# A fused four-layer attention kernel: the first batch of the one-head layer takes its weighted sums of values by seven products

## The chip, the cores and the metric

The kernel runs on one core of one Trainium2 chip. The time is the device time of one execution in microseconds (us); the smaller, the better. The program executes once on all four batches; each engine of the core (TensorE, called PE; VectorE, DVE; ScalarE, ACT; GpSimd, POOL; SyncE, SP, which issues the transfers) runs its own list of instructions in order and waits at semaphores for the others.

## The reference

Four layers follow one another on x of shape (4, 512, 32, 32), all in fp32: an 8-head self-attention, a linear attention with a gate, a 1-head self-attention over layer-normed input, and a 4-head self-attention over group-normed input. The change lies in the third, cut here to what it computes:

```python
def _L2_conv_ref(x, norm_w, w_qkv, b_qkv, w_proj, b_proj):
    xf = jnp.transpose(x, (0, 2, 3, 1)).reshape(b, h * w, c)      # 1024 tokens of 512 channels
    mu = jnp.mean(xf, axis=-1, keepdims=True)
    var = jnp.var(xf, axis=-1, keepdims=True)
    xn = (xf - mu) * jax.lax.rsqrt(var + EPS) * norm_w
    q, k, v = jnp.split(jnp.einsum('bnc,dc->bnd', xn, w_qkv) + b_qkv, 3, axis=-1)
    attn = jax.nn.softmax(jnp.einsum('bqc,bkc->bqk', q, k) * c ** (-0.5), axis=-1)
    out = jnp.einsum('bqk,bkc->bqc', attn, v)
    out = jnp.einsum('bnc,dc->bnd', out, w_proj) + b_proj
    return x + jnp.transpose(out.reshape(b, h, w, c), (0, 3, 1, 2))
```

## The kernel before

All of it is `plain_path`, which runs the layers in sequence and, inside a layer, the four batches. x of a batch is a tile of 128 partitions x 4 channel chunks x 1024 tokens (2 MB). [...] `away(b)` (L573) stores a batch, `back(b)` (L576) fetches one into the tile that the store has freed. Both are issued by SP, in program order.

**Seven products.** A 2 x 2 block matrix product normally takes eight products of quarter size. `seven_products` (from L711) does it with seven, p1 to p7, at the price of sums of quarters: s1 to s4 of the stationary side (made by POOL in `sum_weights`, L693), t1 to t4 of the moving side (made by DVE in `sum_inputs`, L683), and sums of the results, which DVE takes out of PSUM (lines 737, 739, 774, 780). After p1 and p2 of all outputs `o`, it goes through pairs of outputs in the order p6(a), p7(a), p6(a+1), p5(a), p4(a), p7(a+1), p3(a), p5(a+1), p4(a+1), p3(a+1), and after every second one it calls `slot()`. A call `slot()` takes one entry off the list `pieces` and runs it: this is how work of another stage is put between products. `flush()` runs what is left at once.

**The one-head layer, per batch.** (1) q is projected; (2) v is projected (`project_v`: seven slots); (3) `one_head` computes the scores with keys first (`seven_products` with four outputs: ten slots, no slot in its p1 and p2), `exp` (L1237) on ACT, and a running sum `acc` of the exponentials on DVE (L1240); (4) `one_head` computes the weighted sums of values, divides by the row sums (`row_sums`, `invert`) and adds to x (`add_block`, L1263 and L1265). The tile names in the profile are those of the code; `pt`, `pts` are exponentials, `ln` a normed input, `w` a part of the tile `w2`, `qs` the sums of q, `ts` and `w` also sums for stage 4.

**Two ways through stage 4.** Batches 1 to 3 go from L1285 on: seven products written out once more, 2 outputs x 7 products x 4 matmuls = 56 matmuls, with all sums made by DVE in `each` (L1310). Batch 0 takes the branch at L1270: eight output blocks of eight matmuls each (L1277), 64 in all, each block followed by its division and addition, and ahead of each block one entry of the list `parts`.

**The next batch's norm.** `layer_norm(b + 1, tb, ...)` has four steps for each half `tb` of the tokens: `add` (L1557, L1559: three DVE adds of the four channel chunks into `s`), `center` (L1565: a matmul with a matrix of ones gives the mean, `lnsums<-s`; DVE subtracts it, L1567; ACT squares, L1572; DVE adds the squares, L1576), `spread` (L1581: a second matmul for the variance; ACT takes the root, L1583; DVE the reciprocal, L1584), `scale` (four DVE operations, L1589). For batches 1 and 2 these steps are entries of `pieces`; for batch 0 they are entries of `parts`, so they lie in stage 4, and `sum_inputs` of the next batch's input is the last entry there. In batch 0 `pieces` also holds what is left of layer 1 of batch 3, and behind it one entry that stores batch 3 and fetches batch 1.

**What sets the order.** PE's instructions stand exactly in the order in which the code issues them (`tc.manual_schedule` for PE). The other engines' instructions are ordered by a scheduler from priorities (`soon()` raises those of exponentials and of sums out of PSUM), and an engine runs its list strictly in that order. PSUM holds four accumulators (`acc`) and two double tiles (`sc`, used for scores, norm sums and row sums).

Of the kernel before, what the change touches and what calls it, by code (L numbers as in the profile page):

```python
# [18 lines left out]
P = 128  # L19
B = 4  # L20
C = 512
S = 1024
NC = C // P
NT = S // P
TB = 512
NTB = S // TB
# [448 lines left out]
def plain_path(ctx: ExitStack, tc: tile.TileContext, d: dict, out: bass.AP, count):  # L475
# [11 lines left out]
    nc = tc.nc  # L487
# [11 lines left out]
    def acc_tile():  # L499
        return ps_acc.tile([P, TB], F32, tag="acc", name="acc")  # L500

    def two_tile(name):
        return ps_sc.tile([P, 2, TB], F32, tag="sc", name=name)
# [4 lines left out]
    def pt_tile(name):  # L508
        return work.tile([P, 2, TB], F32, tag="pt", bufs=4, name=name)

    def sum_tile(name):
        return work.tile([P, 2, TB], F32, tag="sum", bufs=2, name=name)
# [8 lines left out]
    def q_tiles():  # L521

        return [chunks_tile(f"q{tb}", f"q{tb}") for tb in range(NTB)]

    def chunks_tile(tag, name, bufs=1):
        return work.tile([P, NC, TB], F32, tag=tag, bufs=bufs, name=name)


    def load_wqkv(src):
        t = wpool.tile([P, NC, 3 * C], F32, tag="wqkv", name="wqkv")  # L530
        nc.sync.dma_start(t, src.rearrange("(c p) o -> p c o", p=P))
        return t
# [52 lines left out]
    for c in range(NC):  # L585
# [41 lines left out]
        out=gmat, in_=gmat, pattern=[[-GROUP, P // GROUP], [0, GROUP]],  # L627
# [3 lines left out]
        out=gmat, in_=gmat, pattern=[[GROUP, P // GROUP], [0, GROUP]],  # L631
# [30 lines left out]
    idle = lambda: None  # L662
# [3 lines left out]
    def both(*fs):  # L666
        return lambda: [f() for f in fs]
# [8 lines left out]
    def invert(rd, ps):  # L676

        nc.vector.reciprocal(rd, ps)  # L678
        n, m = next(unit), rd.shape[0]
        for i, t in enumerate((ps, rd)):  # L680
            closing[:] = [nc.vector.tensor_reduce(tops[:m, i, n : n + 1], t, AX.X, ALU.max).ins]

    def sum_inputs(tiles, inputs):  # L683

        t = tiles
        nc.vector.tensor_tensor(t[0], inputs(0, 1), inputs(0, 0), ALU.subtract)
        nc.vector.tensor_tensor(t[1], inputs(1, 1), t[0], ALU.subtract)
        nc.vector.tensor_tensor(t[2], inputs(1, 1), inputs(0, 1), ALU.subtract)
        last = nc.vector.tensor_tensor(t[3], inputs(1, 0), t[1], ALU.subtract)
        summed[:] = [last.ins]  # L690
        return t
# [522 lines left out]
        while parts:  # L1214
            parts.pop(0)()

    def one_head(b, q, ws, acc, xn, sums, v, scale, bias, room, between, parts):

# [6 lines left out]
        pts = [pt_tile("pt") for _ in range(4)] + [sum_tile("pt") for _ in range(2)]  # L1228
        pts += [wide[:, 2 * i : 2 * i + 2, :] for i in range(2)]

        order = [j for o in range(NC) for j in (o, o + NC)]
        pts = dict(zip(order, pts))
# [20 lines left out]
        def row_sums():  # L1253
            rows = two_tile("rowsum")
            for t in range(NTB):
                nc.tensor.matmul(
                    rows[:, t, :], lhsT=ones, rhs=acc[:, t, :], start=True, stop=True
                )
            return rows

        def add_block(m, tb, t, source, quotient):

            nc.vector.tensor_tensor(t, source, quotient, ALU.mult)  # L1263
            xv = x[:, m, bass.ts(tb, TB)]
            nc.vector.scalar_tensor_tensor(xv, t, bias[:, m : m + 1], xv, ALU.add, ALU.add)  # L1265

        flush()
        between()

        if parts:  # L1270
            rds = chunks_tile("q0", "rd")
            for k, (qb, m) in enumerate(itertools.product(range(NTB), range(NC))):
                if parts:
                    parts.pop(0)()
                out = acc_tile()
                for i, j in enumerate(order):
                    nc.tensor.matmul(  # L1277
                        out, lhsT=v[j // 2][:, j % 2, bass.ts(m, P)], rhs=pts[j][:, qb, :],
                        start=(i == 0), stop=(i == NT - 1),
                    )  # L1280
                if k == 0:
                    rows = row_sums()
                if m == 0:
                    invert(rds[:, qb, :], rows[:, qb, :])
                add_block(m, qb, rds[:, NTB + k % 2, :], out, rds[:, qb, :])  # L1285
            return

# [3 lines left out]
        d, e = temps[:2], temps[2:]  # L1293
        quarter = lambda t: t.rearrange("p a (r m) -> p (a r) m", m=n)
        ws = [quarter(t) for t in (xn[1][:, 2:4, :], room[1][:, :2, :], room[1][:, 2:4, :])]
# [70 lines left out]
        rows = row_sums()  # L1366
# [291 lines left out]
    with tc.manual_schedule(engines={mybir.EngineType.PE}):  # L1658
# [8 lines left out]
        for b in range(B):  # L1667
            vt = v_tiles()
            if b > 0:
                pieces.extend(linear_attention(b - 1, lambda i: vt[i]))  # L1670
            q, k = project_qkv(
                wqkv0, "bqkv0", lambda tb: xs[b][:, :, bass.ts(tb, TB)], vt,
                lambda: chunks_tile("ot", "ws"), first=(b == 0),
                between=outputs_bias,
            )
# [20 lines left out]
        def normed_tiles(b):  # L1696

            if b % 2 == 0:
                t = work.tile([P, NTB, NC, TB], F32, tag="k", name="ln")
                return [t[:, tb, :, :] for tb in range(NTB)]  # L1700
            return [chunks_tile("xn", "ln", 2) for _ in range(NTB)]
# [11 lines left out]
        xn = normed_tiles(0)  # L1713
# [37 lines left out]
        spare = [w2[:, NC + 2 * i : NC + 2 * i + 2, :] for i in range(4)]  # L1751
        normed = lambda xn: lambda j, tb: xn[tb][:, 2 * j : 2 * j + 2, :]
        made = []
        for b in range(B):
            q = q_tiles()
            vt = v_tiles()
            after = normed_tiles(b + 1)

            def sums():
                if b == 0:  # L1760
                    made.extend(sum_inputs(spare, normed(xn)))
                return made

            half = NC // 2
            seven_products(
                half,
                lambda i, j, o: gq[:, 2 * j : 2 * j + 2, bass.ts(i * half + o, P)],
                normed(xn),
                lambda i, o: uq[:, i * half + o : i * half + o + 1],
                lambda i, tb, o: q[tb][:, i * half + o, :],  # L1770
                sums,
                slots=2,
            )

            pair = lambda t, i: t[:, 2 * i : 2 * i + 2, :]
            halves = work.tile([P, 2, 2, TB], F32, tag="os", name="qs")
            third = work.tile([P, 2, TB], F32, tag="oi", name="qs")
            places = [halves[:, 0], halves[:, 1], third, pair(q[1], 0)]
            sum_weights(places, lambda i, j: pair(q[i], j))
            if b == 0:  # L1780
                pieces.append(lambda: (away(B - 1), back(1)))
            parts = []
            if b + 1 < B:
                (add0, *n0), (add1, *n1) = [layer_norm(b + 1, tb, after) for tb in range(NTB)]
            if b == 0:

                parts = [
                    both(add0, n0[0]), idle, both(*n0[1:], add1), idle, n1[0], idle,
                    both(*n1[1:]), lambda: sum_inputs(spare, normed(after)),
                ]  # L1790
            elif b + 1 < B:
                pieces.extend([
                    add0, n0[0], idle, n0[1], n0[2], add1, n1[0], idle, n1[1], n1[2],
                ])
            else:
                first = chunks_tile("ot", "gn")
                loaded3 = load_bias(
                    d["bv3"], d["wo3n"], [after[1][:, 2 * i : 2 * i + 2, :] for i in range(2)]
                )
                loads3 = []  # L1800
                pieces.extend([
                    *group_norm(0, 0, first),
                    lambda: loads3.append(weighted_bias("bo3", loaded3)),
                ])
            project_v(vt, hv, normed(xn), made, wpool.tile([P, NC, C], F32, tag="wo", name="ws"))
            one_head(
                b, q, places, work.tile([P, 2, TB], F32, tag="ou", name="acc"), xn, made, vt,
                float(C) ** -0.5, bo2,
                after if b == B - 1 else [w2[:, NC : 2 * NC, :], w2[:, 2 * NC :, :]],
                lambda: b + 1 < B or loads3.insert(0, load_wqkv(d["wqkv3"])), parts,  # L1810
            )
            if 0 < b < B - 1:
                sum_inputs(spare, normed(after))
            away(b)
            back((b + 2) % B)
            if b + 1 < B:
                xn = after
        wqkv3, bo3 = loads3
# [9 lines left out]
        for b in range(B):  # L1828
            vt = v_tiles()

            q, k = project_qkv(
                wqkv3, "bqkv3", lambda tb: ready[tb], vt,
                lambda: wpool.tile([P, NC, C], F32, tag="wo", name="ws") if b == 0
                else chunks_tile("ot", "ws"),
            )
# [85 lines left out]
```

## Time and profile before

| what | value |
|---|---|
| runs | 2452.09, 2451.55, 2450.80 us; median 2451.55 |
| the profiled execution | 2450.76 us, of which 2449.0 from first to last instruction |
| 1-head layer, batch 0: scores | 1043.21 to 1093.49, 50.28 us |
| batch 0: values | 1093.49 to 1153.58, 60.09 us |
| batch 1: q, then v | 1153.58 to 1205.34, 51.76 us |
| batch 1: scores | 1205.34 to 1254.26, 48.92 us |
| batch 1: values | 1254.26 to 1304.18, 49.92 us |
| batch 2: scores, values | 48.92 us, 49.92 us |

The stages are read off PE's timeline: each begins with the first matmul of its line. The scores of batch 0 hold a last piece of layer 1 (1.7 us of matmuls), its values the norm of batch 1. A timeline line gives the start, the length of the merged run, engine, line, operation, output and inputs, shapes and count, and in brackets the idle time before it with what ended that. A source matmul in fp32 appears as two records. PEld, the loading of stationary operands, overlaps the matmuls.

### The profile page before, as it was taken

Reading aid. Unit: us, or ns where it says so; the run is one execution under the profiler, and the core shown is the slowest. Engines: PE = TensorE matmul, PEld = TensorE weight load, DVE = VectorE, ACT = ScalarE, POOL = GpSimd, SP = SyncE. Lnnn points to the kernel's source line nnn. Section 1 sums busy time; section 2 is a strip of 40 time slices with the busy share of each in tenths; the row PEclk is TensorE's granted clock in tenths of the full one; section 3 lists DMA queues with packets and bytes.
Section 4 is the critical chain, followed back from the end, with each engine's and each line's share of the span. In section 5 each row is a group of like instructions: output and inputs, shape, how many; then the busy total and the mean of one; then the engine's idle time right before and its main releaser. Section 6 shows DMA issues by size and latency. Waiting matters only on the chain.

```text
span 2449.0 us, 24662 instructions
## 1 busy us (share of the span) xinstructions
PE 2433.3 (99%) x10098; PEld 1225.7 (50%) x10098; DVE 1506.1 (61%) x1798; ACT 704.6 (29%) x864; POOL 251.1 (10%) x240
## 2 busy tenths in 40 slices
PE   9999999999999999999999999999999999999999
PEld 4544544453455344644645446445556456555653
DVE  3677577757775788656595774763554554445344
ACT  1454144415531653221211201112321430332132
POOL 4001100110010001101103021021010001002000
PEclk9999999999999999999999999999999999999999
DMA  5000020002000301011001010110010001001001
GB/s 185 7 12 18 5 78 10 18 5 79 19 9 13 130 23 48 5 69 39 31 1 69 5 74 13 52 69 18 35 69 1 18 35 52 1 35 35 1 22 45
DMA packets 28959, 88.64 MB, mean 36 GB/s; under 512 B 2508, under 2 KB 10188, under 8 KB 25895
## 3 DMA queue, kind: packets, MB, share of 16 engines
q1 hardware_dynamic: 28838, 87.00, 9.9%
q8 instruction: 81, 1.33, 0.2%
q14 instruction: 40, 0.32, 0.0%
HBM read 60.59 MB, written 25.35 MB: 35 GB/s over the span
## 4 chain that ended last, share of the span: by engine, by line
PE 99%; DVE 1%; ACT 0%; issue 0%; DMA 0%; SPq 0%; DVEq 0%
PE acc L707 20%; PE acc L832 12%; PE acc L967 9%; PE acc L982 9%; PE sc L936 9%; PE sc L931 9%; PE acc L839 8%; PE acc L1084 7%; PE acc L1316 6%; PE acc L1277 2%; PE feat L641 1%; PE acc L1018 1%; PE acc L641 1%; PE upd L1520 1%; PE acc L1454 1%; PE xt L1425 1%
## 5 line engine op out<-in xcount | busy, mean ns | idle before, releaser
L941 ACT ACTIVATE pt<-sc 128x1024 f32<-128x1024 f32 x384 | 379.2, 1022 | 541.2 <-PE sc L936 304.0
L950 DVE TENSOR_TENSOR sum<-sum,pt 128x1024 f32<-128x1024 f32 x256 | 314.6, 1229 | 159.0 <-ACT pt L941 146.5
L967 PE MATMUL acc<-pt,v 64*64 64x512 f32 x2048 | 247.6, 591 | 0.0
L931 PE MATMUL sc<-q,k 64*64 64x512 f32 x2048 | 245.0, 591 | 1.1 <-ACT pt L941 1.1
L982 PE MATMUL acc<-pt,v 128*128 128x512 f32 x512 | 240.8, 594 | 0.0
L936 PE MATMUL sc<-q,k 128*128 128x512 f32 x512 | 239.9, 594 | 0.0
L707 PE MATMUL acc<-t,ws 128*128 128x512 f32 x384 | 173.9, 594 | 0.0
L695 POOL TENSOR_TENSOR ws<-wqkv 128x256 f32<-128x256 f32 (+1 forms) x40 | 39.7, 992 | 1307.1 <-PE acc L1018 523.2
L947 DVE TENSOR_TENSOR sum<-pt 128x1024 f32<-128x1024 f32 x64 | 78.0, 1219 | 137.4 <-ACT pt L941 137.4
L982 PEld LDWEIGHTS acc<-pt,v 128*128 128x128 f32 x512 | 96.8, 190 | 125.1 <-issue 121.4
L936 PEld LDWEIGHTS sc<-q,k 128*128 128x128 f32 x512 | 97.1, 191 | 115.9 <-issue 92.7
L967 PEld LDWEIGHTS acc<-pt,v 64*64 64x64 f32 x2048 | 78.3, 133 | 142.5 <-issue 140.3
L931 PEld LDWEIGHTS sc<-q,k 64*64 64x64 f32 x2048 | 77.3, 133 | 140.9 <-issue 131.9
L707 PEld LDWEIGHTS acc<-t,ws 128*128 128x128 f32 x384 | 72.6, 190 | 86.5 <-issue 85.0
L746 ACT COPY v<-acc 128x512 f32<-128x512 f32 x24 | 14.0, 585 | 308.6 <-PE acc L832 308.6
L678 DVE RECIPROCAL rd<-acc 128x512 f32<-128x512 f32 (+1 forms) x24 | 80.5, 3353 | 29.1 <-PE acc L1018 29.1
L832 PE MATMUL acc<-ws,t 128*128 128x256 f32 x384 | 87.3, 380 | 0.0
L839 PE MATMUL acc<-qs,w 128*128 128x512 f32 x192 | 86.6, 593 | 0.0
L839 PE MATMUL acc<-q,ln 128*128 128x512 f32 x192 | 85.8, 593 | 0.0
L1084 PE MATMUL acc<-ot,wo 128*128 128x256 f32 x336 | 80.7, 383 | 2.7 <-ACT ou L1103 2.7
L737 DVE TENSOR_TENSOR v<-acc,v 128x512 f32<-128x512 f32 x72 | 49.5, 689 | 51.5 <-PE acc L832 51.2
L746 ACT COPY q<-acc 128x512 f32<-128x512 f32 x40 | 23.4, 585 | 197.1 <-PE acc L707 197.1
(326 smaller groups left out, 3476.0 us busy)
## 6 DMA issues: line engine op xcount, KB each, us to landing
home<-x SPq DMA_DIRECT2D x8, 2048.0 KB
x<-home SPq DMA_DIRECT2D x8, 2048.0 KB
out<-x SPq DMA_DIRECT2D x32, 256.0 KB
rds<-quotients SPq DMA_DIRECT2D x30, 256.0 KB
rds<-quotients SPq DMA_DIRECT2D x7, 1024.0 KB
x<-in_x SPq DMA_DIRECT2D x3, 2048.0 KB
wo<-in_wo SPq DMA_DIRECT2D x3, 1024.0 KB
w<-in_w SPq DMA_DIRECT2D x1, 3072.0 KB
```

Source lines behind the costliest of these rows:

```text
L678: nc.vector.reciprocal(rd, ps)
L707: nc.tensor.matmul(ps, lhsT=w[:, m, :], rhs=x[:, m, :], start=start, stop=stop, skip_group_check=True)
L832: nc.tensor.matmul(ps[:, bass.ts(r, C // 2)], lhsT=x[:, m, bass.ts(2 * o + r, P)], rhs=w[:, m, :], start=(start and r == 0), stop=stop, sk ...
L839: nc.tensor.matmul(ps, lhsT=x[:, m, bass.ts(o, P)], rhs=w[:, m, :], start=start, stop=stop, skip_group_check=True,)
L931: nc.tensor.matmul(ps[half(h), s, :], lhsT=key(g, i)[half(s), half(h)], rhs=q[qb][half(s), g, :], start=True, stop=True,)
L936: nc.tensor.matmul(ps[:, s, :], lhsT=key(g, 2 * i + s), rhs=q[qb][:, g, :], start=True, stop=True)
L941: exps.append(nc.scalar.activation(pt, ps, AF.Exp, scale=scale).ins)
L950: adds.append(nc.vector.tensor_tensor(acc, acc, pt, ALU.add).ins)
L967: nc.tensor.matmul(outs[qb, g][r][half(s), :], lhsT=v[i // 2][half(r), i % 2, g * P + s * hd : g * P + (s + 1) * hd], rhs=pt[half(r), s, : ...
L982: nc.tensor.matmul(outs[qb, g][0], lhsT=v[j // 2][:, j % 2, bass.ts(g, P)], rhs=pt[:, s, :], start=(j == 0), stop=(j == NT - 1),)
L1084: nc.tensor.matmul(ps[i][:, bass.ts(o, n)], lhsT=w[:, m, bass.ts(o, P)], rhs=t[:, m, :], start=(start and m + o == 0), stop=(stop and m == ...
L1316: nc.tensor.matmul(ps[i, o], lhsT=w[m][:, bass.ts(o, P)], rhs=t[m], start=(start and m == 0), stop=(stop and m == 3), skip_group_check=True,)
```

## The change

Batch 0 no longer has a way of its own. The branch with 64 matmuls goes, so `one_head` takes seven products for every batch. The steps of the norm of batch 1 become entries of `pieces`, behind the entry that stores batch 3 and fetches batch 1, in the order that batches 1 and 2 use. `sum_inputs` for the next batch now follows `one_head` in batch 0 as it did in batch 1 and 2.

```diff
-    def one_head(b, q, ws, acc, xn, sums, v, scale, bias, room, between, parts):
+    def one_head(b, q, ws, acc, xn, sums, v, scale, bias, room, between):
...
         flush()
         between()
-
-        if parts:
-            rds = chunks_tile("q0", "rd")
-            for k, (qb, m) in enumerate(itertools.product(range(NTB), range(NC))):
-                if parts:
-                    parts.pop(0)()
-                out = acc_tile()
-                for i, j in enumerate(order):
-                    nc.tensor.matmul(
-                        out, lhsT=v[j // 2][:, j % 2, bass.ts(m, P)], rhs=pts[j][:, qb, :],
-                        start=(i == 0), stop=(i == NT - 1),
-                    )
-                if k == 0:
-                    rows = row_sums()
-                if m == 0:
-                    invert(rds[:, qb, :], rows[:, qb, :])
-                add_block(m, qb, rds[:, NTB + k % 2, :], out, rds[:, qb, :])
-            return
...
             if b == 0:
                 pieces.append(lambda: (away(B - 1), back(1)))
-            parts = []
             if b + 1 < B:
                 (add0, *n0), (add1, *n1) = [layer_norm(b + 1, tb, after) for tb in range(NTB)]
-            if b == 0:
-
-                parts = [
-                    both(add0, n0[0]), idle, both(*n0[1:], add1), idle, n1[0], idle,
-                    both(*n1[1:]), lambda: sum_inputs(spare, normed(after)),
-                ]
-            elif b + 1 < B:
                 pieces.extend([
                     add0, n0[0], idle, n0[1], n0[2], add1, n1[0], idle, n1[1], n1[2],
                 ])
...
-                lambda: b + 1 < B or loads3.insert(0, load_wqkv(d["wqkv3"])), parts,
-            )
-            if 0 < b < B - 1:
+                lambda: b + 1 < B or loads3.insert(0, load_wqkv(d["wqkv3"])),
+            )
+            if b < B - 1:
                 sum_inputs(spare, normed(after))
```

## The prediction

> **What bounds the kernel now.** I read the page's shares and its chain of waits first, then TensorE's timeline of the stretch that the change rewrites, then stage windows, then the DMA queue.
>
> ```profile
> span 2449.0 us, 24662 instructions
> PE 2433.3 (99%) x10098; PEld 1225.7 (50%) x10098; DVE 1506.1 (61%) x1798; ACT 704.6 (29%) x864; POOL 251.1 (10%) x240
> PE 99%; DVE 1%; ACT 0%; issue 0%; DMA 0%; SPq 0%; DVEq 0%
> ```
>
> PE has no gaps to give back: a matmul removed is time won, a PE wait added is time lost. The length of one matmul record (about 593 ns) is not its price. Records overlap, and the timeline gives the step:
>
> ```profile
> 1071.18 1.88 PE L839 MATMUL acc<-qs,w 128*128 128x512 f32 x4
> 1072.89 1.88 PE L839 MATMUL acc<-q,w 128*128 128x512 f32 x4
> ...
> 1093.49 1.02 PE L1565 MATMUL lnsums<-s,ones 128*128 128x512 f32 x2
> 1094.35 5.31 PE L1277 MATMUL acc<-pt,v 128*128 128x512 f32 x12
> 1099.50 1.88 PE L1277 MATMUL acc<-pts,v 128*128 128x512 f32 x4
> ```
>
> Four records step 1.71 to 1.72 us, so one costs 0.429; a matmul in the source is two records. The values stages of batch 0 (plain) and batch 1 (seven products), by stage window:
>
> ```profile
> 1093.49:1153.58 60.09, 60.09 (x142) 26.66 (x141) 48.20 (x54) 9.07 (x13) 2.33 (x2) 1.00 0.00 0
> 1254.26:1304.18 49.92, 49.92 (x117) 22.00 (x116) 41.43 (x56) 2.67 (x4) 5.12 (x5) 1.00 0.00 0
> ```
>
> Columns: stage, length, then busy PE, PEld, DVE, ACT, POOL. Both are PE from end to end. Batch 0 checks as (128 + 4 + 8) x 0.429 = 60.1: values, row sums, norm sums. Batch 1 is (112 + 4) x 0.429 = 49.8.
>
> [...] The trace has 0.68 to 0.69, but starts of independent ones lie 0.60 apart, and I use that. [...] After its 4.8 us opening wait the trace does show two matmuls per us, and four from 10 us on, though the granted-clock column stays 1.00:
>
> ```profile
> 8.00:9.00 1.00, 1.00 (x2) 0.33 (x1) 0.00 (x0) 0.00 (x0) 0.00 (x0) 1.00 1.03 375
> 10.00:11.00 1.00, 1.00 (x4) 0.47 (x3) 0.00 (x0) 0.00 (x0) 0.00 (x0) 1.00 1.06 401
> ```
>
> So about 5.3 us passed at half rate there: 2.7 us lost.
>
> **The change, part by part.** *Removed and added on PE.* Values fall from 128 records to 112. The eight norm records stay, now inside scores. 60.09 - 49.92 - 8 x 0.429 = 6.7 us saved if nothing waits.
>
> *The norm moves to where its input is not there yet.* The piece that stores x3 and fetches x1 (`away`, `back`) is unchanged and now stands directly ahead of the norm's pieces. In batch 0 eight pieces of layer 1 are left ahead of it; seven go into project_v's slots, the eighth into slot 1 of scores, away/back into slot 2. So the first adds (`s<-x`) fall in slot 3, the mean matmul (`lnsums<-s`) in slot 4, after p5 of o = 1. The built order of instructions confirms it: on PE the mean matmul stands after the `qs,w` at 1071.18, so PE reaches it at 1072.89. PE's order is fixed, so it stops there. When is x1 there?
>
> ```profile
> 1064.50 0.34 SPq L573 DMA_DIRECT2D home<-x  x1
> 1070.90 0.34 SPq L576 DMA_DIRECT2D x<-home  x1
> ...
> 2038.73 0.34 SPq L576 DMA_DIRECT2D x<-home  x1
> ```
>
> ```profile
> 2046.90 0.69 DVE L1605 BATCH_NORM_STATS2 st<-x 128x6 f32<-128x512 f32 x1 [1.41 <-DMA x<-home]
> ```
>
> SP's order is unchanged; the store waits for the layer-1 update of x3, as before. The fetch is issued at 1070.90. The same transfer later served a DVE that waited for it 8.17 us after issue, so x1 is usable at 1079.07. Three dependent adds: 2 x 0.72 + 0.69 = 2.1, to 1081.2. **First stall: 1081.2 - 1072.9 = 8.3 us.** Before, the adds came at 1080.65 by chance of order, and their matmul at 1093.49: no wait.
>
> *Behind the waiting instructions.* On PE: p4, p3 of o = 1 and the whole second half of scores. On DVE, `s<-x` waits with the centring and the joins of p4, p3 (L737) behind it, on which ACT's exponentials wait.
>
> *DVE then owes more than PE.* In the built order DVE does, between the first norm's sum and the end of the second's: 24 operations 512 wide (4 centring, 3 squares, 4 scaling, 3 adds of the second sum, 10 joins and adds of the products), 4 weight-sum adds 1024 wide (step 1.13), 2 of 256 (0.34), one reciprocal (step 3.27):
>
> ```profile
> 1074.83 0.69 DVE L737 TENSOR_TENSOR pt<-acc,pt 128x512 f32<-128x512 f32 x1
> 1077.13 1.22 DVE L1240 TENSOR_TENSOR acc<-acc,pt 128x1024 f32<-128x1024 f32 x1
> 1078.31 0.69 DVE L774 TENSOR_TENSOR pt<-pt,acc 128x512 f32<-128x512 f32 x1
> 1112.64 3.34 DVE L1584 RECIPROCAL rstd<-rstd 128x512 f32<-128x512 f32 x1
> ```
>
> 24 x 0.60 + 4 x 1.13 + 2 x 0.34 + 3.27 = 22.9 us, from 1082.4 (mean matmul 0.86 and 0.3 to be seen) to 1105.3. PE meanwhile has the mean and variance matmuls (1.7) and ten products of four records (17.2): it stands before the second mean matmul at 1100.1. **Second stall: 5.2 us.**
>
> *The second norm's variance.* From 1105.3 DVE does 2 x 0.34 and 4 x 0.60 of sums for the seven products, 4 centring, 2 joins, a 256-wide sum, 3 squares and a 1024-wide add: 3.1 + 7.0 = 10.1, to 1115.4. PE has one mean matmul and two products, 4.3, and stands at 1109.7. **Third stall: 5.7 us.**
>
> *Hidden, and by what.* The rest of the sums on DVE (about 17 us) end at about 1132; the products that read them start about 1131, p6's own near 1122. Batch 1 has the same order here, and its values stage holds 0.1 us of idle time. ACT gets two more table loads (2 x 1.28) beside its 29% load: the first rstd is ready near 1092, its reciprocal's turn comes at 1093. Without that 1 us cover it would move the second stall one for one. The four input sums for the next batch go into the finishing adds, as in batch 1. The norm issues no DMA. POOL's order is unchanged, its next block sums become free as in batch 1, and the fetch of x2 for batch 1's own norm keeps its distance from the end of batch 0.
>
> *Clock.* No wait over 4.8 us is in this trace, so what PE loses after a stall is an estimate: from 0 ([...] DVE is late anyway) to 5 (the opening's 2.7 us twice). [...] I take 2: after the first stall part of the 2.7 shows through the joins that DVE waits for.
>
> Sum against the profiled execution (2450.76, of it span 2449.0): -6.7 + 8.3 + 5.2 + 5.7 + 2.0 = +14.5, to 2465.3. The median of the runs shown is 0.8 higher: **2466.0**.
>
> **Rivals.**
> *Only the transfer costs.* DVE catches up after the first stall: -6.7 + 8.3 = +1.6, 2453.2. For it: batch 1 runs a norm through scores with DVE at 33.67 of 48.92 us and PE idle 0.7. Against: there the first norm lies in project_v and the second's sum ends before scores; here both lie within 12 products.
> *The norm is covered (the other side, faster).* One mechanism: x1 usable before slot 4, and DVE's queue ahead of PE's. Then 6.7 us are won: 2444.8. It decides as long as all waits together stay under 6.7 us. It would need the 2 MB store and fetch in under 6 us after 1064.50; the fetch is only issued 6.4 us after it.
> *Each stall also costs the full cold start*: 8.1 for the clock in place of 2: 2472.1. [...] Against: a slow PE eats into the second and third stall, which DVE sets.
>
> **Numbers.** Three stalls as forecast 0.80, transfer only 0.08, covered 0.04, cold each time 0.08. The range: low, no clock loss, data at 1077.5 (1.6 earlier) and DVE 5 us less behind, 2457.4; high, 5 for the clock and 2 more from DVE, 2471. I give 2457 to 2471; transfer only, covered and cold each time (0.20) lie outside. This measurement can tell some 0.2% (4.9 us) from no change: faster 0.04, same 0.08, slower 0.88.
>
> **What would show it.** Right: PE idle of about 8, 5 and 6 us before the mean matmul of the first, the mean and the variance matmul of the second norm; `s<-x` waiting for the DMA near 1071 + 8; a values stage of 50 us; two matmuls per us after the first stall. Wrong: no DMA wait at `s<-x`, or the second and third stall missing, which would mean that I overcount DVE's queue; or a values stage that waits for its sums, which I have at nothing.

## The result, and the profile after

| kernel | median | lowest to highest |
|---|---|---|
| before | 2451.18 us (4 runs) | 2450.40 to 2452.09 |
| after | 2465.93 us (4 runs) | 2464.61 to 2467.74 |

The ratio is 1.0061, with a 95% interval from 1.0043 to 1.0078: slower by 14.75 us on the medians. The profiled execution took 2467.74 us, of which its span is 2466.0; it is the slowest of the four, and 16.98 us above the profiled execution of before.

The page of the kernel after, first its span, then shares of busy time, then the shares of the chain of waits:

```profile
span 2466.0 us, 24680 instructions
PE 2432.7 (99%) x10082; PEld 1221.0 (50%) x10082; DVE 1527.8 (62%) x1840; ACT 708.1 (29%) x868; POOL 251.9 (10%) x240
PE 97%; DVE 1%; DMA 0%; ACT 0%; issue 0%; SPq 0%; DVEq 0%; ACTq 0%
```

PE has 16 fewer records than before and a span that is 17 us longer, and its share of the chain fell from 99 to 97%. Its busy time hardly fell: matmuls at half clock count as busy (1.00 of each us below, at a granted clock of 0.50).

At the start of batch 0's scores this execution is 1.24 us ahead of that of before (its opening wait was 0.57 us shorter, 4.23 against 4.80, and its slow start was shorter as well: four records per us from 9 us on, before from 10 us on), so times are compared from there. TensorE's timeline of the kernel after:

```profile
1069.93 1.88 PE L839 MATMUL acc<-qs,w 128*128 128x512 f32 x4
1080.31 2.08 PE L1546 MATMUL lnsums<-s,ones 128*128 128x512 f32 x2 [8.50 <-DVE s L1540]
1082.17 3.62 PE L839 MATMUL acc<-q,w 128*128 128x512 f32 x4
1085.59 2.28 PE L839 MATMUL acc<-q,ln 128*128 128x512 f32 x4
1087.70 3.60 PE L839 MATMUL acc<-qs,w 128*128 128x512 f32 x8
...
1100.58 1.88 PE L839 MATMUL acc<-qs,w 128*128 128x512 f32 x4
1107.37 2.08 PE L1546 MATMUL lnsums<-s,ones 128*128 128x512 f32 x2 [4.92 <-DVE s L1540]
1109.24 2.39 PE L839 MATMUL acc<-q,w 128*128 128x512 f32 x4
1111.47 1.88 PE L839 MATMUL acc<-q,ln 128*128 128x512 f32 x4
1117.31 2.08 PE L1562 MATMUL lnsums<-sq,ones 128*128 128x512 f32 x2 [3.96 <-DVE sq L1557]
1119.18 3.40 PE L1297 MATMUL acc<-pt,v 128*128 128x512 f32 x6
```

Three waits, each at a matmul of the norm, each for a DVE sum. Each is followed by records at twice their step: after the first, four `q,w` take 3.42 us (1082.17 to 1085.59), where four records at full rate take 1.72. Windows of 1 us of the kernel after (length, busy PE, PEld, DVE, ACT, POOL, then the granted clock) show it, and the last line is the whole values stage of batch 0:

```profile
1082.00:1083.00 1.00, 1.00 (x2) 0.34 (x1) 0.58 (x1) 0.00 (x0) 0.00 (x0) 0.50 0.00 0
1085.00:1086.00 1.00, 1.00 (x2) 0.41 (x2) 0.17 (x1) 0.03 (x1) 0.00 (x0) 0.50 0.00 0
1086.00:1087.00 1.00, 1.00 (x3) 0.35 (x2) 1.00 (x2) 0.38 (x1) 0.00 (x0) 0.81 0.00 0
1087.00:1088.00 1.00, 1.00 (x4) 0.41 (x3) 1.00 (x4) 1.00 (x2) 0.00 (x0) 1.00 0.00 0
```

```profile
1119.18:1169.77 50.59, 50.59 (x118) 22.26 (x117) 43.92 (x57) 1.86 (x3) 5.12 (x5) 0.99 0.00 0
```

Values fell from 60.09 to 50.59 us without a wait. The loss lies in scores. What released the first sum is in the DMA queue and on DVE:

```profile
1069.66 0.34 SPq L576 DMA_DIRECT2D x<-home  x1
```

```profile
1078.11 0.69 DVE L1538 TENSOR_TENSOR s<-x 128x512 f32<-128x512 f32 x1 [3.72 <-DMA x<-home]
1078.84 1.42 DVE L1540 TENSOR_TENSOR s<-s,x 128x512 f32<-128x512 f32 x2
...
1106.63 0.68 DVE L1540 TENSOR_TENSOR s<-s,x 128x512 f32<-128x512 f32 x1
...
1116.57 0.68 DVE L1557 TENSOR_TENSOR sq<-sq 128x512 f32<-128x512 f32 x1
```

Only the first adds wait for the transfer, 8.45 us after its issue (the kernel keeps x in two tiles, `bufs=2`; the other batches rest in DRAM). The sums of 1106.63 and 1116.57 have no bracket: DVE came to them late because it was busy. From the start of scores (1041.96, before 1043.21) to the end of values (1169.77, before 1153.58) the kernel took 127.81 us, before 110.37: 17.44 more, all of the difference between the two profiled executions.

### The profile page after: what moved, and what is told of

It is laid out like the page before. It is cut to its first block, busy times and chain, and to the rows that moved or that the text cites. A ratio compares the mean times of both kernels' runs of the same rounds, so it can differ in the third digit from the quotient of the medians.

```text
span 2466.0 us, 24680 instructions
## 1 busy us (share of the span) xinstructions
PE 2432.7 (99%) x10082; PEld 1221.0 (50%) x10082; DVE 1527.8 (62%) x1840; ACT 708.1 (29%) x868; POOL 251.9 (10%) x240
## 4 chain that ended last, share of the span: by engine, by line
PE 97%; DVE 1%; DMA 0%; ACT 0%; issue 0%; SPq 0%; DVEq 0%; ACTq 0%
PE acc L707 20%; PE acc L832 11%; PE acc L967 9%; PE acc L982 9%; PE sc L936 9%; PE sc L931 9%; PE acc L1297 8%; PE acc L839 8%; PE acc L1084 7%; PE feat L641 1%; PE acc L1018 1%; PE acc L641 1%; PE upd L1501 1%; PE acc L1435 1%; PE xt L1406 1%; PE kv L641 1%
## 5 line engine op out<-in xcount | busy, mean ns | idle before, releaser
L695 POOL TENSOR_TENSOR ws<-wqkv 128x256 f32<-128x256 f32 (+1 forms) x40 | 39.7, 991 | 1305.7 <-PE acc L1018 523.3
```

## Experiments

Each ratio is to the kernel before, run beside it on the same chip (medians 2450.66 to 2450.85). Differences to the kernel after join two series of runs, between which the median of the kernel before differs by some 0.5 us. Where a trace is compared with that of the kernel after, "the stretch" is the time from the start of batch 0's scores to the end of its values: 110.37 us before, 127.81 after. Together they ask three things: what the move of the norm costs without the seven products, what makes the three waits, and whether another place for the norm keeps the saving.

### The norm moved, eight products kept (norm_moved_eight)

```diff
+        if b == 0:
+            ...
+            for k, (qb, m) in enumerate(itertools.product(range(NTB), range(NC))):
...
+            return
```

The branch with 64 matmuls comes back for batch 0, without entries of the norm in it.

> Only the norm is moved into the slots of scores; the values of batch 0 keep eight products. Theory (a transfer wait, then DVE's queue twice, then the clock): 8.7 for the transfer, about 4.5 and 2.3 us for the second and third wait, since the sums for the seven products are not in DVE's queue, and about 4 for the clock: some 2470 us. Rival one, the second and third wait come from the sums for the seven products alone: 8.7 and 3.1 for the clock, about 2463. Rival two, the seven products themselves cost the time and the move nothing: about 2451.

2471.35 us (2470.89 to 2472.90), ratio 1.0085 (1.0071 to 1.0099). Its timeline on TensorE:

```profile
1080.87 2.08 PE L1562 MATMUL lnsums<-s,ones 128*128 128x512 f32 x2 [8.61 <-DVE s L1556]
...
1105.98 1.12 PE L1562 MATMUL lnsums<-s,ones 128*128 128x512 f32 x2 [3.18 <-DVE s L1556]
1115.43 1.12 PE L1578 MATMUL lnsums<-sq,ones 128*128 128x512 f32 x2 [3.19 <-DVE sq L1573]
```

The move alone costs 20.6 us, near the theory's 2470; both rivals fall, though the two later waits were expected at 4.5 and 2.3. The seven products, on top of it, win 5.4 us by the medians (2471.35 - 2465.93) and 2.8 in the stretch (130.64 against 127.81). That they win less than the 6.9 of 16 records goes with the later waits, 3.2 us each here against 4.9 and 4.0 in the kernel after. DVE's way from the first mean to the second norm's sum is 1.95 us shorter here: two 256-wide sums (0.68) are missing ahead of that sum, and one 1024-wide add (1.13) stands behind it, at 1105.85.

### The transfer taken away (norm_of_x0)

```diff
-        x = lambda c: xs[b][:, c, bass.ts(tb, TB)]
+        src = xs[0] if b == 1 else xs[b]
+        x = lambda c: src[:, c, bass.ts(tb, TB)]
```

Batch 1's norm reads the tile of batch 0, which is there all along; so batch 1 is computed from another input.

> As the changed kernel, but the norm of batch 1 reads x0, which lies in its tile all along, so nothing of it waits for the transfer; batch 1 is then computed from the wrong input. Theory: the first wait (8.7) and its clock loss (3.1) go, part of DVE's queue stays since its work is the same: 2448 to 2454 us. Rival, all three waits come from the late transfer, the later two as its echo: all 17 us of waits and 6 of clock go, about 2444.5. Rival, the waits are DVE's own whatever the transfer does: above 2460.

2457.55 us (2456.82 to 2458.12), ratio 1.0028 (1.0017 to 1.0038): 8.4 below the kernel after, and above what I expected. TensorE:

```profile
1072.13 1.02 PE L1547 MATMUL lnsums<-s,ones 128*128 128x512 f32 x2
...
1082.10 1.12 PE L1563 MATMUL lnsums<-sq,ones 128*128 128x512 f32 x2 [2.08 <-DVE sq L1558]
...
1096.71 1.13 PE L1547 MATMUL lnsums<-s,ones 128*128 128x512 f32 x2 [3.18 <-DVE s L1541]
...
1106.08 1.13 PE L1563 MATMUL lnsums<-sq,ones 128*128 128x512 f32 x2 [3.12 <-DVE sq L1558]
```

The first mean matmul waits no more, but five others do: these three and two in values (0.33 and 1.89), 10.6 us in all. I had taken DVE's lag to begin with the transfer. It does not: with the data there from the start, twelve products are too short for DVE's share of the norm, and this alone exceeds the 6.7 us of saving. The transfer would be enough for a loss too: 8.7 us of wait in the kernel after, clock not counted. This is a sum; no run has the transfer's wait without DVE's.

### Keeping PE busy through the waits (warm_first, warm_all)

```diff
+    warm = lambda ps, n: [
+        nc.tensor.matmul(ps, lhsT=ones, rhs=t_warm[0], start=True, stop=True) for _ in range(n)
+    ]
...
+            if b == 1:
+                warm(t["ps"][:, 1, :], (9, 0)[tb])
```

Nine useless matmuls stand ahead of the first mean matmul; in warm_all five and four more stand ahead of the matmuls of the second and third wait.

> As the changed kernel, with nine matmuls (7.7 us) of no use put ahead of the first mean matmul, so that PE is busy while it would wait 8.7 us. Theory (the half clock after the wait costs time because DVE waits for PE's joins): about 3 us faster than the changed kernel, 2463. Rival, DVE sets the pace after the first wait and the slow clock is hidden: no change, 2466.

> As before, with nine, five and four useless matmuls ahead of the three matmuls that wait, each a little shorter than the wait. Theory: the records after the three waits lost 3.1, 1.5 and 1.7 us to the half clock, so up to 6.3 us faster than the changed kernel, about 2460. Rival, clock loss only hides inside waits: 2466, or slower by what the useless matmuls add.

warm_first: 2462.23 us (2460.69 to 2462.76), ratio 1.0044 (1.0030 to 1.0058). warm_all: 2463.73 (2462.80 to 2464.51), ratio 1.0052 (1.0038 to 1.0066). TensorE in warm_first:

```profile
1073.63 7.89 PE L1533 MATMUL lnsums<-ln,ones 128*128 128x512 f32 x18
1082.07 1.13 PE L1553 MATMUL lnsums<-s,ones 128*128 128x512 f32 x2 [0.55 <-DVE s L1545]
1083.03 1.88 PE L839 MATMUL acc<-q,w 128*128 128x512 f32 x4
...
1105.31 1.50 PE L1553 MATMUL lnsums<-s,ones 128*128 128x512 f32 x2 [3.39 <-DVE s L1545]
1106.62 3.24 PE L839 MATMUL acc<-q,w 128*128 128x512 f32 x4
```

The `q,w` after the first wait take 1.88 in place of 3.62 us, and the kernel wins 3.7 us by the medians, about as expected. In the two traces the stretch is shorter by more, 6.7 us (121.15 against 127.81): 3.0 of it are the records after the first wait, the rest comes from later waits that are shorter (3.39 and 2.22 against 4.92 and 3.96) and from the last of them, after which no half clock follows. warm_first itself begins batch 0's scores 2.0 us later than the kernel after, ahead of anything that was changed. So half clock after the first wait, with what it does to the later ones, costs some 4 to 7 us. To fill the two later waits as well won nothing more, against my expectation; the kernel is 1.5 slower than warm_first. My reading, which no run tests alone, is that the lost clock there is for the most part time in which PE would have waited for DVE anyway. Nor do the fillers (7.7 us) fit exactly: DVE's second sum is done at 1103.61, and behind the five fillers PE takes it at 1104.41.

### DVE's queue made shorter (no_running_sum, sums_on_pool)

```diff
-            if len(taken) > 1:
+            if len(taken) == 2 or (len(taken) > 2 and b > 0):
                 nc.vector.tensor_tensor(acc, acc if len(taken) > 2 else taken[0], pt, ALU.add)
```

```diff
-        each(s1, weights(1, 0), weights(1, 1), ALU.add)
-        each(s2, s1, weights(0, 0), ALU.subtract)
-        each(t1, inputs(0, 1), inputs(0, 0), ALU.subtract)
-        each(t2, inputs(1, 1), t1, ALU.subtract)
+        each(s1, weights(1, 0), weights(1, 1), ALU.add, pool)
+        each(s2, s1, weights(0, 0), ALU.subtract, pool)
+        each(t1, inputs(0, 1), inputs(0, 0), ALU.subtract, pool)
+        each(t2, inputs(1, 1), t1, ALU.subtract, pool)
```

In sums_on_pool s3 and s4 move too, for batch 0 alone.

> The changed kernel, but batch 0 makes only the first of its seven running-sum adds of 1024 (acc plus pt): this leaves out six terms of the softmax denominator in batch 0, so its output there is another; nothing is put on POOL. It tests the DVE queue without a second engine. Theory (the second and third wait are DVE's queue): three or four of these adds stand between the first and the second norm sum and one more before the variance add, at 1.13 us each, so the second wait of 5.1 falls to about 1 and the third by about 1; with less cold clock after them the time is 2459 to 2461 us beside 2465.9. Rival (a chain through ACT or PE sets those waits, not the length of the queue): no change, 2464 to 2467.

> The changed kernel with the sums that batch 0's seven products of values need (s1 to s4 and t1, t2) made by POOL, so that they leave DVE's queue. My theory (the second and third wait of PE are DVE's own queue): the third wait of 4.1 us shrinks by about 3, as two 256-wide and four 512-wide sums of the forecast's 10.1 us are gone from ahead of the variance matmul (2 x 0.34 + 4 x 0.60), and the second changes by under 1; the first stays at 8.5. Time 2461 to 2463 us beside 2465.9 of the changed kernel. Rival (the third wait is the chain centre, square, add with PE and ACT in it, not the queue's length): no change, 2465 to 2467. Rival (POOL's sums come late for the products that read them): PE waits in values, over 2466.

no_running_sum: 2461.34 us (2459.70 to 2461.88), ratio 1.0041 (1.0027 to 1.0055). sums_on_pool: 2469.55 (2468.98 to 2471.25), ratio 1.0079 (1.0065 to 1.0092). TensorE in no_running_sum:

```profile
1105.36 1.12 PE L1546 MATMUL lnsums<-s,ones 128*128 128x512 f32 x2 [1.79 <-DVE s L1540]
...
1112.40 1.13 PE L1562 MATMUL lnsums<-sq,ones 128*128 128x512 f32 x2 [2.48 <-DVE sq L1557]
```

no_running_sum makes the first of batch 0's running-sum adds and leaves out the others. Four adds fewer (4 x 1.13 = 4.5) stand between the two norm sums, and four short sums that the scheduler moved up (3 x 0.34 + 0.60 = 1.6) stand there in their place. DVE's way from the first mean to the second norm's sum is 21.7 us in place of 24.9, 3.2 shorter, and the second wait fell by 3.1 us, the third by 1.5: the length of DVE's queue sets them. The time is just above the 2459 to 2461 that I expected. sums_on_pool, expected at 2461 to 2463, went the other way: the third wait fell to 1.8 us as hoped, but the second grew, and PE waited 1.7 us for a join at 1099.11 as well. TensorE in sums_on_pool:

```profile
1111.18 2.08 PE L1548 MATMUL lnsums<-s,ones 128*128 128x512 f32 x2 [8.37 <-DVE s L1542]
```

DVE in sums_on_pool, between the first and the second norm sum:

```profile
1105.45 2.28 DVE L1239 TENSOR_TENSOR acc<-acc,pt 128x1024 f32<-128x1024 f32 x1
1107.65 1.74 DVE L1542 TENSOR_TENSOR s<-s,x 128x512 f32<-128x512 f32 x1
```

and POOL beside it:

```profile
1103.27 1.71 POOL L1291 TENSOR_TENSOR ts<-pt 128x512 f32<-128x512 f32 x1
1104.94 3.91 POOL L1291 TENSOR_TENSOR w<-pt,ts 128x512 f32<-128x512 f32 x2
```

The 1024-wide add takes 2.28 us where it took 1.22, the 512-wide one 1.74 where it took 0.68: each lost just over 1 us while POOL was adding. Between the two norm sums such excesses come to 5.6 us, and the second wait grew from 4.9 to 8.4. The two above lose 1.06 us each beside adds of 512 (1.26 us each alone); others, most of them beside adds of 256 (0.72 alone), lose about 0.5, and POOL's own adds grow, two of them to 3.91 us. What makes the two engines slow each other the trace does not show. I had not reckoned with this loss, neither in the theory nor in the rivals of that run.

### The norm in other places (seven_norm_in_values, norm_late_pool, norm_mid_pool)

All three keep the seven products. `part()` calls are put between the products of batch 0's values, and the norm's steps become their entries:

```diff
-                pieces.extend([
-                    add0, n0[0], idle, n0[1], n0[2], add1, n1[0], idle, n1[1], n1[2],
-                ])
...
+                    parts = [
+                        both(add0, n0[0]), idle, idle, idle, both(n0[1], n0[2], add1), idle, idle, idle,
+                        n1[0], idle, idle, both(n1[1], n1[2]),
+                    ]
```

This list is that of seven_norm_in_values; batches 1 and 2 keep theirs in `pieces`. norm_late_pool has the last two entries two products and one product later (the expectation says two to three) and batch 0's s1 to s4 on POOL. norm_mid_pool instead puts the first half's add and mean into slots 6 and 8 of scores, and has the same four sums on POOL. The expectations name t1 and t2 too; these stayed on DVE.

> Seven products in batch 0's values as in the changed kernel, but the steps of the norm of batch 1 stand between the products of values, where they stood before the change. My theory: the transfer has landed long before, so the waits of 8.5 and 5 us in scores are gone; what is left is DVE, which in values then has the sums of the products and the norm, about 62 us of work against PE's 53 (50 of products and 3.4 of norm matmuls): waits of 4 to 10 us, 2450 to 2457 us. Rival (seven products are themselves dearer in batch 0 than the matmuls that they save): no better than the changed kernel, 2463 or more. Rival (DVE's load does not matter once the transfer is there): no waits, the full saving of 6.7, 2444.

> As the run with the norm between the products of values, with the second half's norm two to three products later and with the sums s1 to s4, t1, t2 of batch 0's values on POOL, which takes about 5 us off DVE. My theory (placement and DVE's load decide, not the seven products): waits of 1 to 4 us, 2445 to 2449 us, faster than both kernels. Rival (DVE is still too full, or POOL's sums come late): waits over 6.7 us, 2451 or more.

> The first half's adds and mean matmul stay in scores, but four slots later than in the changed kernel, when the transfer has landed; everything behind the mean stands between the products of values; sums s1 to s4, t1, t2 on POOL. My theory: the first wait is gone because x1 is there (four slots are over 10 us), and DVE's work is spread over both stages: waits of 0 to 4 us, 2444 to 2449 us. Rival (DVE's queue in scores is already full without the norm): a wait of 3 us or more before the first mean matmul, 2449 or more.

| run | median | ratio, 95% interval |
|---|---|---|
| seven_norm_in_values | 2454.66 us | 1.0016 (1.0009 to 1.0022) |
| norm_late_pool | 2456.87 us | 1.0025 (1.0016 to 1.0035) |
| norm_mid_pool | 2450.29 us | 0.9999 (0.9991 to 1.0008) |

seven_norm_in_values came within its theory. The other two did not: both were expected faster than the kernel before, at 2449 us at most. In seven_norm_in_values one wait is left, at the second half's mean matmul in values:

```profile
1132.07 2.04 PE L1553 MATMUL lnsums<-s,ones 128*128 128x512 f32 x2 [8.31 <-DVE s L1547]
```

DVE had two reciprocals of row sums and one of the norm, 3.35 us each, ahead of that sum. The ten records after the wait lost another 3.2 us to half clock. In norm_late_pool this wait is 2.0 us and values end 2.7 us earlier than before (86.42 us after the store of x3 is issued, before 89.08). Then the time comes back at the next stage, in the projection of batch 1's q:

```profile
1163.86 8.93 PE L707 MATMUL acc<-w,ws 128*128 128x512 f32 x16 [5.93 <-DVE w L687]
```

The sums of the norm's output (L686 to L689) were not ready: 5.9 us of waiting and 1.9 of half clock (8.93 in place of 7.03). The norm came late, but that is not all of it:

```profile
1157.03 2.28 DVE L686 TENSOR_TENSOR w<-ln 128x1024 f32<-128x1024 f32 x1
1158.19 2.24 POOL L696 TENSOR_TENSOR ws<-ws,w 128x512 f32<-128x512 f32 x1
```

From the scaling of the norm at 1148.77 to the sum that PE waits for, DVE's operations took 5.7 us longer than the same ones elsewhere (L686 took 1.22 before), while POOL made its sums for that projection (L695 to L698). By these lengths POOL's sums account for about the whole wait; no run moves them. So whether this place for the norm, 2.7 us ahead of the kernel before until then, could keep its lead was not tried.

norm_mid_pool lies between the two: no first wait, waits of 0.4, 2.5 and 0.4 us in values, and a time that can't be told from before. So its theory failed although the first wait went as it said, and its rival, a wait before the first mean, did not come either. The wait of 2.5 us:

```profile
1122.79 5.40 PE L1299 MATMUL acc<-ts,ln 128*128 128x512 f32 x8 [2.48 <-DVE ln L1262]
```

### Order and load on DVE (norm_mid_order, norm_mid_dve_order, norm_mid_t4_pool)

```diff
-        for t in range(NTB):
-            invert(quotients[t], rows[:, t, :])
+        invert(quotients[0], rows[:, 0, :])
+        if b > 0:
+            invert(quotients[1], rows[:, 1, :])
         for o in range(2):
             finish(0, 0, o, e[o], ps[1, o])
+        if b == 0:
+            invert(quotients[1], rows[:, 1, :])
```

This is norm_mid_pool to norm_mid_order. norm_mid_dve_order has s1 to s4 back on DVE; norm_mid_t4_pool puts t4 on POOL as well.

> The run with the first mean late in scores, with one more edit for batch 0: the reciprocal of the second half's row sums stands behind the two divisions and additions that need only the first half's, so the two accumulators come free 5 us earlier. In that run PE waited 2.5 us for one of these divisions and then ran at half clock for about 2 us. My theory (order in DVE's queue, not its load, makes that wait): the wait is gone, 2446 to 2448 us. Rival (DVE is simply full there, so the wait moves to the next reader): 2449.5 to 2451.

> The same with the sums s1 to s4 of batch 0's values back on DVE. In the runs with sums on POOL many DVE operations on two SBUF inputs took 1.21 us in place of 0.68, or 1.75 in place of 1.22, while POOL was busy. My theory (POOL's work costs DVE about as much as it takes off, 16 sums of 256 at 0.34, some 5 us): the time is within 2 us of the run with POOL. Rival (POOL's help is real): slower by 3 us or more.

> The run norm_mid_order with one more set of sums (t4 of batch 0's values, four of 512) made by POOL, which is idle there between 1101 and 1135 us. In norm_mid_order PE waits 2.5 us for these sums, since DVE has three reciprocals of 3.3 us ahead of them, and runs at half clock afterwards (5.3 us for eight records in place of 3.6). My theory (DVE's load is the last thing that holds PE here; POOL's contention is small while DVE does reciprocals and reads PSUM): that wait and its cold clock are gone, 2445.5 to 2447.5 us, faster than both kernels. Rival (every shift only moves the wait to the next reader of DVE): 2449 to 2451.

| run | median | ratio, 95% interval |
|---|---|---|
| norm_mid_order | 2450.05 us | 0.9996 (0.9988 to 1.0005) |
| norm_mid_dve_order | 2456.08 us | 1.0020 (1.0012 to 1.0028) |
| norm_mid_t4_pool | 2450.59 us | 1.0000 (0.9992 to 1.0009) |

The rival was right in all three. TensorE in norm_mid_order:

```profile
1117.27 3.70 PE L1299 MATMUL acc<-w 128*128 128x512 f32 x8 [0.42 <-DVE ln L1309]
1120.81 3.60 PE L1299 MATMUL acc<-ts,ln 128*128 128x512 f32 x8
1124.24 1.02 PE L1558 MATMUL lnsums<-s,ones 128*128 128x512 f32 x2
1127.77 5.31 PE L1299 MATMUL acc<-ts,v 128*128 128x512 f32 x8 [2.51 <-DVE ts L1291]
```

The wait of 2.5 us at `ts,ln` that norm_mid_pool had is gone and a wait of 2.5 us at `ts,v`, two groups later, has taken its place. With t4 on POOL, DVE shows in norm_mid_t4_pool:

```profile
1104.86 1.75 DVE L1291 TENSOR_TENSOR w<-pts,ts 128x512 f32<-128x512 f32 x1
1106.53 1.75 DVE L1550 TENSOR_TENSOR s<-x 128x512 f32<-128x512 f32 x1
1108.21 1.75 DVE L1291 TENSOR_TENSOR pt<-pt 128x512 f32<-128x512 f32 x1
```

and TensorE:

```profile
1121.48 5.09 PE L1299 MATMUL acc<-w 128*128 128x512 f32 x8 [4.69 <-DVE ln L1309]
```

POOL's four adds took 2.4 us (4 x 0.60) off DVE and cost it 4.3: four operations ran 1.07 us longer, these three and one more. The reciprocals kept their 3.34 to 3.35 us, but POOL was done at 1109.41, before the first of them began (1111.08). The wait of 2.5 us is gone and that at `acc<-w` has grown from 0.4 to 4.7. Yet norm_mid_dve_order, with nothing on POOL, is 6.0 us slower than norm_mid_order: there 16 sums of 256 stand on DVE, s3 behind the reciprocals, and PE waits 9.1 us for it:

```profile
1124.19 3.78 PE L1298 MATMUL acc<-pt,w 128*128 128x512 f32 x4 [9.13 <-DVE w L1291]
```

So, in these runs, POOL helps where PE waits for the result of just those sums and hurts where DVE's two-input work is what PE waits for. No version can be told to be faster than the kernel before. Moving the norm back into values, with nothing else, takes the loss from 14.8 us to 3.9 (seven_norm_in_values); with half of it late in scores and s1 to s4 on POOL nothing is left of the loss. The 6.7 us of saved matmuls did not come out in any version's time, and in each trace PE waits for DVE.

## Why the prediction was right

The forecast was 2466.0 us, measured 2465.93. Term by term, from the starts in TensorE's timeline; a wait is the start of the matmul less the start of the group before it and that group's 1.72:

| step | forecast | profile after |
|---|---|---|
| matmuls saved, norm moved | -6.7 | -6.7 (values 49.9 without half clock) |
| first stall | 8.3 | 8.66 (1080.31 - 1069.93 - 1.72) |
| second stall | 5.2 | 5.07 (1107.37 - 1100.58 - 1.72) |
| third stall | 5.7 | 4.12 (1117.31 - 1111.47 - 1.72) |
| half clock | 2.0 | 6.31 |
| sum | +14.5 | +17.4 |

**What held.** The place of all three waits, their cause and their order. The transfer: usable 8.45 us after its issue, forecast 8.17. DVE's queue up to the second norm's sum: 22.9 us forecast (its 0.60 is the distance between the starts of independent 512-wide DVE operations in fp32, as at 1080.05 and 1080.65 in the trace of before), 24.9 measured (1082.42 to 1107.31), of it 1.4 idle behind PE, most of it at half clock. PE was later by as much, so the difference came out the same. That this stall is DVE's queue was an inference in the forecast; no_running_sum shows it.

**What was mis-sized: the clock.** That half clock would follow a stall was my estimate; in the trace of before only the opening shows it, after a wait of 4.80 us. Each of the three waits put PE on half clock, which cost 3.10, 1.53 and 1.68 us in records (10, 6 and 10 records by their starts, less 0.429 each). I had 2.0 for all, with 5 as the upper end. Part of it takes the place of a wait: the 1.53 lost after the second wait made PE come that much later to the third, which is why that stall is 1.6 shorter than forecast. In the forecast's terms the clock is thus worth some 4.8 (6.31 - 1.53), near its upper end. The 2.0 had stood for part of a cold start after the first stall alone; the first wait cost more than that, and the two shorter ones brought half clock too. Stalls and clock together are 24.2 us, forecast 21.2.

**How the median still fits.** The profiled execution lies 1.8 us above the median of its kernel, so the agreement of the medians to 0.1 us is luck within a spread of 3 us; the sum of the steps is 2.9 us short of the execution that it describes. The other executions have no trace, and where they lose 1 to 3 us less stays open. In the traces of this document batch 0's scores begin between 1041.71 and 1043.95 us, though no edit stands ahead of them; the kernel after begins them early, at 1041.96, so its 1.8 us were not lost there.

**What was hidden at nothing** held: values have no wait, nor has the projection of q behind them, for which POOL makes its sums, and the first square root, behind a table load of 1.28 us on ACT, was ready at 1094.22, its reciprocal began at 1094.62. The cover of 1 us was 0.4.

**The rivals.** *Only the transfer* fell: two waits remain without the transfer, and more. *Covered* fell with it: norm_of_x0 leaves 10.6 us of waits even with the data there. That rival needed DVE's queue to be ahead of PE's as well, as the forecast said. *Full cold start each time* (8.1) was too high: 6.3 in records, and some 4.8 once the shorter third wait is set against it. Its reason against itself, that a slow PE eats into a stall that DVE sets, is what happened at the third.

## What to carry to other kernels

A step that another engine does beside a full PE was free here where that engine's whole queue between two of its PE instructions was no longer than PE's work between them; where it was longer, PE waited. In the kernel after DVE took 24.9 us from the first mean to the second norm's sum, PE was through its own work 19.9 us into them (1102.30) and waited 5.07; in values, with DVE busy for 43.92 of 50.59 us, it waited nowhere. So count both, operation by operation, at the new place. To price a wait, add the half clock after it (3.10, 1.53 and 1.68 us here), and then look whether the next wait absorbs it. Before giving work of a late engine to a third one, look at whether the two slow each other down (DVE's adds by 0.5 or 1.07 us beside POOL's), and at which single result PE waits for.

## What the hardware showed that was not expected

- Half clock follows waits shorter than the opening one of before, 4.80 us. After 3.96 (the kernel after), 3.39 (warm_first) and even 2.51 us (norm_mid_order) of waiting PE ran two to three records per us at a granted clock of 0.50; after the last, eight records took 5.31 us in place of 3.60. A wait of 3.12 us in norm_of_x0 had no such effect, and of two waits of 2.48 us the one in norm_mid_pool had it (5.40 us for eight records) and the one in no_running_sum had not. Two waits of 8.37 us in sums_on_pool cost 1.5 and 3.1 us in the records behind them. So length alone decides neither whether nor for how long; what else does, these runs do not show.
- The granted-clock column read 1.00 through the slow start of the kernel before (two records per us from 5 to 10 us), but 0.50 after the waits named here, where it agrees with the step of the records.
- In sums_on_pool and norm_mid_t4_pool many DVE operations on two SBUF inputs lost 0.5 or 1.07 us each while POOL added; joins that read PSUM kept their 0.68 beside POOL in sums_on_pool, and in the kernels before and after reciprocals kept 3.35 us with POOL adding for up to 2.9 of them.
